# A hybrid attention and mixture-of-experts kernel: Strassen's form for all but three first layers, and three small broadcasts moved from TensorE and VectorE to transfers

## The chip, the cores and the metric

The kernel runs on one core of a Trainium2 chip. The metric is the device time of one execution in microseconds (us), smaller is better; medians of several executions are quoted. A kernel that differs from another by under 2% is classed as "same"; the 95% intervals of the ratios resolve far less than that, so effects of one per cent can still be studied, and this document is about such effects. All executions used here are in the fast state. In the views TensorE is PE (its weight load PEld), VectorE DVE, ScalarE ACT, GpSimd POOL, and SyncE, whose queue issues most transfers, SP. The lines L668 and L669 are those of a helper that records every operation.

## The reference, cut to what matters

The input is 8 maps of 256 channels by 32x32 positions, in f32. Layer 0 is a convolutional attention: queries from every position, keys and values pooled to fewer tokens, 8 heads of 32 channels. Layer 1 is an attention with one head and then 8 experts of three layers, mixed by a gate.

```python
attn = softmax(einsum('bhqd,bhkd->bhqk', q_g, k) * SCALE)      # layer 0
out_att = einsum('bhqk,bhkd->bhqd', attn, v)
...
x = x + _L0_conv_ref(_gn(x), ...)                              # the residual of layer 0
t = _to_tokens(x)
t = t + _L1_attn_ref(_ln_t(t), ...)                            # _ln_t: (v - mean) / sqrt(var + eps), by token
t = t + _L1_ffn_ref(_ln_t(t), ...)
...
h = relu(_bn(einsum('bfd,edh->bfeh', x, W1) + b1, ...))        # experts: first layer
h = relu(_bn(einsum('bfeh,ehk->bfek', h, W2) + b2, ...))       # second
y = einsum('bfeh,ehd->bfed', h, Wo) + bo                       # third
return einsum('bfed,fe->bfd', y, w)                            # w: the gates, softmax over the 8 experts
```

## The kernel before

Layer 0's attention runs in 384 score steps, 12 for each of 32 "units" (8 maps, 2 channel halves, 2 halves of the positions). The work of layer 1 and of the next maps is filling work: TensorE does it in the gaps between score steps. A small model of time inside the program, `Flow`, decides while the program is written in which order every engine gets its instructions. It keeps a clock for each engine, a believed duration for each instruction and a believed landing for each transfer. On the chip each engine then works strictly in that order.

```python
MARGIN = 1.5
NEAR = {"DVE": 1.5, "ACT": 2.0, "POOL": 1.0, "SP": 10.0}
LANDING = 9.5
...
        self.now[engine] = end = start + cost          # in Flow.note, for every instruction
        lag = 0.15
        if "dma" in op:
            lag = 3.0 if engine == "SP" else LANDING    # when a transfer's data are believed there
        for n in {*outs, self.key(out)}:
            self.ready[n] = max(self.ready.get(n, 0.0), end + lag)
...
        if engine == "PE":                              # in Flow.runnable: may a matmul fill this gap?
            until = max(pe, self.free("sc") - 0.5)
            return (... and at + MARGIN <= until and slot <= until)
```

A `yield ve(rec)` in a thread means: go on when `rec` is believed ready for VectorE. The sums of the exponentials and the division by them, in each unit:

```python
            rec = T(work, [P, 512], "rec")              # at the end of sums(n, pairs)
            f.act.activation(rec, total, AF.Copy, accum_out=hi[...])
            return rec

        def normalise(b, c, sl, rec, n):
            att = atts[b, c][:, sl]
            yield ve(rec)
            f.ve.reciprocal(rec, rec)                   # 128 x 512: each of 4 rows stands there 32 times
            f.ve.tensor_tensor(att, att, rec, ALU.mult)
            yield act(rec)
            f.act.activation(rec, rec, AF.Copy, accum_out=lo[...])
```

The reciprocals of the deviations of `_ln_t` (48 broadcasts for the 8 maps), the residual of layer 0, and the gates:

```python
            for g in range(0, tiles, 4):                # in scale_tokens(src, n)
                ...
                f.pool.tensor_tensor(diag, ident[...], r[...], ALU.mult)           # a diagonal for each tile
                yield pe(diag, tag="sm")
                f.pe.matmul(rb[...], lhsT=kit.ones, rhs=diag[...])                 # spreads it over the partitions
                yield ve(rb)
                f.ve.tensor_tensor(d, d, rb[...].to_broadcast([P, 2, m * P]), ALU.mult)
...
                    f.sp.dma_start(xt, x[b, m * P : (m + 1) * P, sl])              # in project(b)
                    ...
                    f.ve.scalar_tensor_tensor(xt, ps, bias[:, m : m + 1], xt, ALU.add, ALU.add)
                    f.sp.dma_start(t1[b][:, m, sl], xt)
...
                for e in range(NE):                     # in gates()
                    f.pe.matmul(ps, lhsT=sel[:, e * P : (e + 1) * P], rhs=gt[:, sl], start=True, stop=True)
                    f.act.activation(gb[:, e, sl], ps, AF.Copy)
```

Of the kernel before, what the change touches and what calls it, by code (L numbers as in the profile page):

```python
# [35 lines left out]
NEAR = {"DVE": 1.5, "ACT": 2.0, "POOL": 1.0, "SP": 10.0}  # L36
BUFS = {"sm": 2, "sx": 1}
PACE2 = 8.0
LANDING = 9.5
# [616 lines left out]
class Flow:  # L656
# [90 lines left out]
    def note(self, engine, op, ins, args, kwargs):  # L747
# [35 lines left out]
        if "dma" in op:  # L783
            lag = 3.0 if engine == "SP" else LANDING
# [95 lines left out]
def attention(tc, kit, f, outer, ended, nb, consts, x, t1, t2, hn, bounds, vecs, q_t, kv_t, proj_t, gqk_t, wqk, wqkv, vecs1, w1_d, w1c, gate_d, wrc, vecs2, bnvec):  # L880
# [6 lines left out]
    with ExitStack() as ctx:  # L887
# [38 lines left out]
        pjw = weight(proj_t, "v", 256, l1)  # L926
# [27 lines left out]
        def mix():  # L954
# [66 lines left out]
            bdt = T(l1, [P, 2, P], "diag4")  # L1021
# [40 lines left out]
        def pool(*tiles):  # L1062
            return "POOL", tiles, None

# [49 lines left out]
        first, large, whole, pooled = {}, [], [], []  # L1114

        def first_diagonals():

            middle = T(l1, [P, 2, P], "rec1")
            rest = T(work, [P, 4, 512], "pt", bufs=6).rearrange("p a (b q) -> p (a b) q", q=P)
            first["diag"] = middle, rest  # L1120
            for c in range(2):
                yield act(vec, mid)
                f.act.activation(middle[:, c, :], ident, AF.Copy, scale=mid[:, c * 4 : c * 4 + 1])
                for i, tap in enumerate((0, 1, 2, 3, 5, 6, 7, 8)):
                    yield act(vec)
                    f.act.activation(rest[:, 8 * c + i, :], ident, AF.Copy, scale=dw(c, 0, tap))

        def first_maps(xp):


            for m in (2, 3, 0, 1):
                c = m % 2
                if m == 2:
                    p, acc = pmap, T(work, [P, NK], "acc", bufs=3)
                elif m == 3:
                    p = T(work, [P, 4, 512], "pt", bufs=6).rearrange("p j q -> p (j q)")
                    acc = T(work, [P, NK], "acc", bufs=3)
                else:
                    both = T(work, [P, 4, 512], "pt", bufs=6).rearrange("p j q -> p (j q)")
                    p = both  # L1140
                    acc = T(work, [P, 4, 512], "pt", bufs=6).rearrange("p j q -> p (j q)")
                for t in (p, acc):
                    if t is not pmap:
                        f.split(t, 512, HW)
                first[m] = p, acc
            for s0, w in KEY_SLICES:
                if s0 >= HW:
                    yield until(lambda: pooled)
                for m in (2, 3, 0, 1):
                    c = m % 2  # L1150
                    p, acc = first[m]
                    src = source(xp, s0, w)
                    yield pe(src, tag="sm")
                    ps = small()
                    for k in range(2):
                        f.pe.matmul(
                            ps[:, :w],
                            lhsT=kvw[:, k, m * P : (m + 1) * P],
                            rhs=src[:, k, :],
                            start=k == 0,  # L1160
                            stop=k == 1,
                        )
                    f.act.activation(p[:, s0 : s0 + w], ps[:, :w], AF.Copy)
                    for s, n in enumerate(SIDES):
                        a, z = max(OFFS[s], s0), min(OFFS[s] + n * n, s0 + w)
                        if a < z and (m >= 2 or s):
                            f.act.activation(
                                acc[:, a:z],
                                ps[:, a - s0 : z - s0],
                                AF.Identity,  # L1170
                                bias=db(c, s),
                                scale=mid[:, c * 4 + s : c * 4 + s + 1],
                            )
                if s0 == 512:
                    large.append("maps")
                    f.spawn(first_keys(), 5)
            whole.append("maps")

        def first_keys():
# [3 lines left out]
            for half in range(2):  # L1183
                for m in range(2):
                    p, acc = first[m]
                    pin = p[:, : n * n].rearrange("p (h w) -> p h w", h=n)
                    yield pe(p[:, : n * n], middle, rest, tag="sm")
                    ps = small()
                    pout = ps.rearrange("p (h w) -> p h w", w=n)
                    for i, tap in enumerate((4, 0, 1, 2, 3, 5, 6, 7, 8)):  # L1190
                        dy, dx, y0, y1, x0, x1 = windows(tap, n)
                        y0, y1 = max(y0, 16 * half), min(y1, 16 * half + 16)
                        f.pe.matmul(
                            pout[:, y0 - 16 * half : y1 - 16 * half, x0:x1],
                            lhsT=rest[:, 8 * m + i - 1, :] if i else middle[:, m, :],
                            rhs=pin[:, y0 + dy : y1 + dy, x0 + dx : x1 + dx],
                            start=i == 0,
                            stop=i == 8,
                        )
                    f.act.activation(acc[:, half * 512 : half * 512 + 512], ps, AF.Identity, bias=db(m, 0))  # L1200
                large.append(("keys", half))
# [135 lines left out]
        def prepare(b):  # L1337

            xi = xs.pop(b) if b in xs else load_x(b)
            st = T(work, [P, 2, 2, 6], "st")  # L1340
# [34 lines left out]
            if b == 0:  # L1375
                todo.extend([None] * 4)
                yield from first_maps(xp)
            else:
                yield from maps(xp)

            for c in range(2):
                if b == 0:
                    qs[b, c] = T(work, [P, HW], "q", bufs=2)
                for half in range(2):
                    sl = slice(half * 512, half * 512 + 512)
                    yield pe(xi, tag="sm")
# [9 lines left out]
                    q = T(work, [P, 512], "pool") if b else qs[b, c][:, sl]  # L1396
# [3 lines left out]
            made[0] += 1  # L1400
# [37 lines left out]
        def keys_and_values(b):  # L1438
            yield until(lambda: b == 0 or len(done) >= 4 * b + 2 and turn[0] >= 2 * b - 2)
            vts[b] = {}  # L1440
            if b == 0:
                for g in range(2):
                    yield from value_tokens(b, g)
            else:
                for g in range(3):
                    f.spawn(value_tokens(b, g), 2)
# [3 lines left out]
            for g in range(2 if b == 0 else 3):  # L1450
                yield from key_tokens(b, g)
            if b == 0:
                yield from value_tokens(b, 2)
                yield from key_tokens(b, 2)
# [32 lines left out]
        def sums(n, pairs):  # L1487
# [16 lines left out]
            return rec  # L1504

        def normalise(b, c, sl, rec, n):
            att = atts[b, c][:, sl]
            yield ve(rec)
            f.ve.reciprocal(rec, rec)
            f.ve.tensor_tensor(att, att, rec, ALU.mult)  # L1510
            yield act(rec)
            f.act.activation(rec, rec, AF.Copy, accum_out=lo[:, column[n] : column[n] + 1])

        def project(b):
# [3 lines left out]
            for m in range(2):  # L1518
                for half in range(2):
                    sl = slice(half * 512, half * 512 + 512)  # L1520
                    if b == nb - 1:
                        xt = last[:, m, sl]
                    else:
                        xt = T(work, [P, 512], "xr")
                        f.sp.dma_start(xt, x[b, m * P : (m + 1) * P, sl])
                    yield pe(atts[b, 0], atts[b, 1], tag="sm")
# [5 lines left out]
                    yield ve(ps, xt)  # L1532
                    f.ve.scalar_tensor_tensor(xt, ps, bias[:, m : m + 1], xt, ALU.add, ALU.add)
                    if b < nb - 1:
                        f.sp.dma_start(t1[b][:, m, sl], xt)
# [4 lines left out]
        def scale_tokens(src, n):  # L1540
# [3 lines left out]
            for g in range(0, tiles, 2):  # L1544
                yield pe(src, tag="sm")
                ps = small()
                for u in range(2):
                    for c in range(2):
                        o = u * C + c * P
                        f.pe.transpose(ps[:, o : o + P], src[:, c, (g + u) * P : (g + u + 1) * P], ident)  # L1550
# [5 lines left out]
            for g in range(0, tiles, 4):  # L1556
                m = min(4, tiles - g)
                yield pool(r)
                diag = T(l1, [P, m, P], f"diag{m}")
                f.pool.tensor_tensor(  # L1560
                    diag,
                    ident[:, None, :].to_broadcast([P, m, P]),
                    r[:, g : g + m].unsqueeze(2).to_broadcast([P, m, P]),
                    ALU.mult,
                )
                yield pe(diag, tag="sm")
                rb = small()
                f.pe.matmul(
                    rb[:, : m * P], lhsT=kit.ones, rhs=diag.rearrange("p t q -> p (t q)"), start=True, stop=True
                )  # L1570
                yield ve(rb)
                d = src[:, :, g * P : (g + m) * P]
                f.ve.tensor_tensor(d, d, rb[:, None, : m * P].to_broadcast([P, 2, m * P]), ALU.mult)
# [3 lines left out]
        def layer1():  # L1577

            for b in range(nb):
# [3 lines left out]
                yield from scale_tokens(t, HW)  # L1583
# [47 lines left out]
        def outputs():  # L1631

            for i in range(4 * nb):
# [41 lines left out]
                f.spawn(norm(b, q, res), 5)  # L1675
# [3 lines left out]
        def norm(b, q, o):  # L1679

            yield from scale_tokens(o, C)
# [108 lines left out]
        def unit(b, c, sl, n, pairs):  # L1790
            rec = yield from sums(n, pairs)
            yield from normalise(b, c, sl, rec, n)
# [10 lines left out]
        f.finish(lambda: key_parts[0] > 1)  # L1803
# [661 lines left out]
```

## Time and profile before

| | before |
|---|---|
| median time | 3413.8 us (3412.5 to 3414.2) |
| profiled span | 3418.4 us |
| PE without a matmul in flight | 213.6 us |
| PE busy at half clock | 114.6 us |

The last two rows are worked out from the trace: the first is the span less the merged records of matmuls, the second the part of those records that lies where the granted clock is 0.5. Full-clock work is busy time less half of the second row: 3418.4 - 213.6 - 57.3 = 3147.5 us. Any change of the span is then a change of one of three things: work, idle time, or half of the half-clock time.

The prediction shows the engine shares, the stages and the start of this kernel. Two more views matter later. First, the start and the steady attention once more, cut at score steps, so that the same pieces of work can be compared (columns: stretch, length, then busy time and instructions of PE, weight load, DVE, ACT and POOL, then granted clock, share of the DMA engines, GB/s). Steps are counted from 0: before's step 8 is at 163 us, step 48 at 341, the last at 1977:

```profile
0.00:163.00 163.00, 105.03 (x380) 49.30 (x384) 98.75 (x253) 65.45 (x112) 42.16 (x64) 0.83 0.23 58
341.00:1977.00 1636.00, 1546.15 (x8776) 694.98 (x8768) 1253.12 (x2169) 1026.45 (x1219) 363.05 (x426) 0.98 0.58 130
```

Second, the waits in that steady stretch (the engine and what it was to write, what ended the wait, then us in total, times, the longest):

```profile
PE sc L669 <- ACT pt L669: 66.2, 66, 3.9
...
DVE pt L669 <- DMA pt<-pt: 62.5, 27, 7.7
DVE rec L669 <- ACT rec L669: 51.9, 20, 5.7
...
ACT p L669 <- DVE acc L669: 31.4, 14, 5.3
```

TensorE's own largest wait is for the exponentials ("pt") that empty its score banks. VectorE waits for transfers where it adds pairs of exponentials that accumulating transfers have summed, and another 31 us for the loads of the residual ("xr", not shown). Before the reciprocals it waits 52 us for ScalarE's copy into "rec". ScalarE (ACT) waits 31 us for VectorE's taps ("acc", the multiply-adds of the convolution on the maps) to free a map buffer.

### The profile page before, as it was taken

How to read it: one execution, taken by the hardware profiler on the slowest of the kernel's cores; microseconds unless marked ns; L12 is line 12 of the kernel's file. 1: busy time of each engine (PE TensorE's matmuls, PEld its weight loads, DVE VectorE, ACT ScalarE, POOL GpSimd, SP SyncE). 2: the span in 40 equal slices, each digit the busy share in tenths (PEclk: the TensorE clock that was granted, in tenths of full speed). 3: DMA queues.
4: the chain of work that ended last, by engine and by line, in shares of the span. 5: the costliest groups of instructions: out<-in, count | busy, mean ns of one | idle time of the engine just before them, and what ended most of it. 6: DMA issues, size and time to landing. Idle time of an engine off the chain costs nothing.

```text
span 3418.4 us, 39922 instructions
## 1 busy us (share of the span) xinstructions
PE 3204.7 (94%) x15264; PEld 1781.8 (52%) x15264; DVE 2285.8 (67%) x3914; ACT 1675.6 (49%) x2193; POOL 499.0 (15%) x616
## 2 busy tenths in 40 slices
PE   7588899999999899999999989998999999999998
PEld 3232244444444334434434356646777777777776
DVE  6587798888888878888644543216776666666665
ACT  3466667566676576566664523342223333333332
POOL 3122213122141221321211200004000000000000
PEclk9699999999999999999999999999999999999999
DMA  1257565555555655555665663123440000000000
GB/s 48 63 114 165 135 135 115 125 126 123 138 116 122 161 108 128 127 122 129 148 134 132 141 191 124 56 77 132 140 160 31 19 29 27 19 19 19 19 13 20
DMA packets 105032, 337.47 MB, mean 99 GB/s; under 512 B 12976, under 2 KB 38328, under 8 KB 81600
## 3 DMA queue, kind: packets, MB, share of 16 engines
q0 software_dynamic: 24576, 172.51, 25.8%
q1 hardware_dynamic: 76896, 160.35, 13.6%
q8 instruction: 122, 2.00, 0.2%
q10 hardware_dynamic: 3360, 1.97, 0.2%
q14 instruction: 78, 0.64, 0.1%
HBM read 98.33 MB, written 63.97 MB: 47 GB/s over the span
## 4 chain that ended last, share of the span: by engine, by line
PE 74%; DMA 5%; ACT 4%; DVE 2%; issue 2%; POOL 1%; SPq 0%; ACTq 0%; DVEq 0%; POOLq 0%
PE bank L669 25%; PE sm L669 18%; PE y L669 11%; PE sc L669 8%; PE sx L669 6%; PE pv L669 6%; ACT pt L669 3%; DMA pt<-pt 2%; DMA t<-xr 1%; DMA xr<-in_x_dram 1%; DVE acc L669 0%; DMA hn<-hn 0%; DVE pt L669 0%; DVE rec L669 0%; DVE xr L669 0%
## 5 line engine op out<-in xcount | busy, mean ns | idle before, releaser
L669 ACT ACTIVATE pt<-sc 128x2048 f32<-128x2048 f32 (+1 forms) x384 | 720.7, 1877 | 317.1 <-PE sc L669 244.7
L669 PE MATMUL sc<-q,kn 32*128 32x512 f32 (+1 forms) x3072 | 452.4, 659 | 115.5 <-ACT pt L669 114.0
L669 DVE SCALAR_TENSOR_TENSOR acc<-p,vec,acc 128x225 f32<-128x225 f32 (+7 forms) x928 | 528.5, 576 | 35.7 <-ACT acc L669 11.2
L669 PE MATMUL bank<-h,w2e 128*128 128x512 f32 x1024 | 480.5, 595 | 0.0
L669 ACT ACTIVATE h<-bank,bnvec 128x512 f32<-128x512 f32 x302 | 233.1, 772 | 484.5 <-PE bank L669 464.4
L669 DVE TENSOR_TENSOR pt<-pt,pt 128x1024 f32<-128x1024 f32 x320 | 390.0, 1261 | 84.8 <-DMA pt<-pt 82.6
L669 PE MATMUL pv<-pt,vt 128*32 128x512 f32 (+1 forms) x3072 | 422.6, 623 | 0.0
L669 ACT ACTIVATE h<-c,bnvec 128x512 f32<-128x512 f32 x210 | 159.6, 807 | 318.6 <-DVE c L669 318.6
L669 POOL DMA_DIRECT2D pt<-pt x192 | 169.8, 884 | 923.2 <-ACT pt L669 788.8
L669 DVE TENSOR_TENSOR c<-p1c,bank 128x512 f32<-128x512 f32 x105 | 72.2, 688 | 314.9 <-PE bank L669 314.9
L669 PEld LDWEIGHTS sc<-q,kn 32*128 32x128 f32 (+1 forms) x3072 | 117.8, 181 | 311.5 <-ACT pt L669 209.4
L669 PEld LDWEIGHTS bank<-h,w2e 128*128 128x128 f32 x1024 | 194.8, 191 | 153.0 <-issue 141.4
L669 PEld LDWEIGHTS pv<-pt,vt 128*32 128x32 f32 (+1 forms) x3072 | 61.0, 109 | 306.6 <-issue 291.4
L669 POOL TENSOR_TENSOR rstd<-rstd,mhalf 128x4 f32<-128x4 f32 (+2 forms) x88 | 107.0, 1216 | 733.8 <-DVE rstd L669 593.7
L669 DVE TENSOR_TENSOR h<-h,gates 128x1024 f32<-128x1024 f32 x128 | 156.9, 1226 | 71.3 <-DMA h<-h 64.2
L669 PE MATMUL bank<-hn,w1e 128*128 128x256 f32 (+1 forms) x604 | 192.7, 448 | 10.1 <-DMA hn<-hn 10.1
L669 PE MATMUL y<-t,s3e 128*128 128x256 f32 x768 | 187.1, 380 | 0.0
L669 PE MATMUL sm<-p,v 128*128 128x256 f32 x736 | 173.8, 388 | 6.1 <-DVE xr L669 6.1
L669 ACT ACTIVATE p<-sm 128x512 f32<-128x512 f32 (+1 forms) x154 | 89.9, 584 | 173.7 <-PE sm L669 134.2
L669 PE MATMUL sm<-y,t 128*128 128x256 f32 x712 | 169.4, 385 | 2.1 <-ACT p L669 2.1
L669 PEld LDWEIGHTS bank<-hn,w1e 128*128 128x128 f32 x604 | 114.7, 191 | 99.9 <-issue 92.4
L669 PEld LDWEIGHTS sm<-p,v 128*128 128x128 f32 x736 | 139.3, 193 | 49.7 <-issue 24.4
(294 smaller groups left out, 4624.9 us busy)
## 6 DMA issues: line engine op xcount, KB each, us to landing
pt<-pt POOLq DMA_DIRECT2D x160, 1024.0 KB, 7.3
h<-h SPq DMA_DIRECT2D x80, 512.0 KB, 3.4
xi<-in_x_dram SPq DMA_DIRECT2D x16, 512.0 KB, 5.0
t<-t SPq DMA_DIRECT2D x8, 1024.0 KB, 6.9
res<-t SPq DMA_DIRECT2D x32, 256.0 KB, 4.4
t<-res SPq DMA_DIRECT2D x32, 256.0 KB, 2.6
hn<-res SPq DMA_DIRECT2D x32, 256.0 KB, 3.4
hn<-hn SPq DMA_DIRECT2D x16, 512.0 KB, 5.8
```

Source lines behind the costliest of these rows:

```text
L669: ins = fn(*args, **kwargs)
```

## The change

The intent is to take work off TensorE and VectorE. (1) First layers of the experts in Strassen's form (7 products of half size in place of 8) from the fourth on. (2) The gates are spread over the partitions by transfers from DRAM. (3) So are the reciprocals of the deviations. (4) The reciprocals of the attention's sums are taken on 16 columns, where each sum stands once, and spread by a chain of transfers. (5) The residual of layer 0 is added by an accumulating transfer. (6) The start is reordered: keys before values, the score loop after one key group. (7) `Flow` believes another landing. The core of the diff:

```diff
-NEAR = {"DVE": 1.5, "ACT": 2.0, "POOL": 1.0, "SP": 10.0}
+NEAR = {"DVE": 1.5, "ACT": 2.0, "POOL": 1.0, "SP": 1.0}
-LANDING = 9.5
...
-            lag = 3.0 if engine == "SP" else LANDING
+            size = ...                                     # KB
+            lag = 2.0 + 0.0045 * size if engine == "SP" else 1.5 + 0.0078 * size
...
             f.act.activation(rec, total, AF.Copy, accum_out=hi[:, column[n] : column[n] + 1])
-            return rec
+            few = T(work, [P, 16], "few")
+            yield sp(rec)
+            f.sp.dma_start(few, rec[::DH, :].rearrange("j (i k) -> j i k", k=16))
+            return rec, few
...
-            yield ve(rec)
-            f.ve.reciprocal(rec, rec)
+            yield ve(few)
+            f.ve.reciprocal(few, few)
+            yield sp(few)
+            f.sp.dma_start(rows[n].rearrange("j (i k) -> (j i) k", k=16), few)
+            yield sp(rows[n])
+            for j in range(4):
+                f.sp.dma_start(rec[DH * j : DH * j + DH, :], rows[n][j : j + 1, :].to_broadcast([DH, 512]))
+            yield act(few)
+            f.act.activation(few, few, AF.Copy, accum_out=lo[:, column[n] : column[n] + 1])
+            yield ve(rec)
             f.ve.tensor_tensor(att, att, rec, ALU.mult)
-            yield act(rec)
-            f.act.activation(rec, rec, AF.Copy, accum_out=lo[:, column[n] : column[n] + 1])
...
-            for g in range(0, tiles, 4):                   # scale_tokens: the diagonals and their matmuls
-                ...
+            yield sp(r)
+            f.sp.dma_start(row.rearrange("o (p u) -> (o p) u", u=tiles), r)
+            yield sp(row)
+            for o in range(0, n, w):
+                rb = T(l1, [P, w], f"rb{w}")
+                f.sp.dma_start(rb, row[:, o : o + w].to_broadcast([P, w]))
                 yield ve(rb)
...
+                        f.act.activation(xt, ps, AF.Identity, bias=bias[:, m : m + 1])
+                        f.pool.dma_start(out=t1[b][:, m, sl], in_=xt, accum_op=ALU.add)
...
-        f.finish(lambda: key_parts[0] > 1)
+        f.finish(lambda: key_parts[0] > 0)
...
+                if i == 4:
+                    f.finish(lambda: {0, 1}.issubset(whole))   # before score step 4: all of this thread's work
...
-                    f.pe.matmul(ps, lhsT=sel[:, e * P : (e + 1) * P], rhs=gt[:, sl], start=True, stop=True)
-                    f.act.activation(gb[:, e, sl], ps, AF.Copy)
+            f.sp.dma_start(gtd, gt)                        # and 16 broadcasts from it, later
...
+            (first if n1 < 3 else first7)(n1)
```

(Cut: the sums around Strassen's products, moved code, the order of the first maps, argument lists.)

## The prediction

> **What bounds the kernel now.** I read the page's engine shares first, then the busy time by stage, then the groups of instructions by shape, then TensorE's waits, then the timeline of the start. The page's first part:
>
> ```profile
> PE 3204.7 (94%) x15264; PEld 1781.8 (52%) x15264; DVE 2285.8 (67%) x3914; ACT 1675.6 (49%) x2193; POOL 499.0 (15%) x616
> ```
>
> TensorE (PE) is busy for 3205 of 3418 us and the chain that ended last is 74% PE. So every matmul taken away should pay almost in full, and everything else can gain only from the 213 us in which PE is idle. Where these lie is in the stretches I cut by stage (columns: stretch, then PE, weight load, DVE, ACT, POOL busy, clock, DMA share, GB/s): start, early attention, steady attention, the experts' two first layers beside the rest of layer 1, and the experts' steady loop.
>
> ```profile
> 0.00:165.00 165.00, 107.03 (x385) 49.66 (x386) 99.44 (x254) 67.05 (x112) 42.16 (x64) 0.82 0.23 57
> 165.00:500.00 335.00, 286.49 (x1646) 107.61 (x1645) 273.89 (x473) 222.02 (x258) 70.97 (x80) 0.95 0.59 131
> 500.00:2003.00 1503.00, 1432.80 (x8126) 660.95 (x8125) 1133.23 (x1954) 928.95 (x1107) 332.38 (x389) 0.98 0.58 129
> 2003.00:2340.00 337.00, 315.04 (x1031) 187.59 (x1029) 95.33 (x174) 109.73 (x174) 36.51 (x55) 0.97 0.33 118
> 2340.00:3418.00 1078.00, 1063.39 (x4080) 775.97 (x4080) 683.93 (x1062) 347.87 (x542) 16.98 (x29) 0.99 0.14 47
> ```
>
> Subtracting, PE is idle 58, 48.5, 70, 22 and 14.6 us. The start is the worst place for its length, and its clock is 0.82. DVE is at 82% from 165 to 500 us and 75% after, so it is the second bound of the attention. In the start's timeline PE has nothing to do until the first keys are in token order:
>
> ```profile
> 75.96 0.66 PE L669 MATMUL sm<-con,pt 128*128 128x128 f32 x4 [1.25 <-ACT vt L669]
> 89.15 1.95 PE L669 MATMUL sx<-con,kt 128*128 128x128 f32 x4 [12.54 <-ACT kt L669]
> 99.73 2.80 PE L669 MATMUL sm<-con,kt 128*128 128x128 f32 x8 [6.38 <-ACT kt L669]
> 102.46 2.09 PE L669 MATMUL sc<-q,kn 32*128 32x512 f32 x8
> 130.28 2.09 PE L669 MATMUL sc<-q,kn 32*128 32x512 f32 x8 [7.14 <-ACT pt L669]
> 145.80 2.09 PE L669 MATMUL sc<-q,kn 32*128 32x512 f32 x8 [6.43 <-ACT pt L669]
> ```
>
> The first scores start at 102 us, and then they stall for 6 to 7 us at a time. The code says why: the start holds all six "pt" buffers (one of diagonals, one for a value map, four for the two key maps and their sums), and the scores' exponentials need the same six.
>
> **What the skill says.** (1) The Trainium skill, "TensorE: Matmul & The Clock Gate", section "What's actually happening": after about 3.4 us of idleness TensorE's clock falls to half. The trace agrees: after the 12.54 us gap the clock reads 0.50 and the same eight score matmuls take 2.09 us, against 1.14 us in warm stretches. (2) "VectorE: DVE Perf Modes", section "First, the fixed hardware budget": a reciprocal is an iterative divide with a repeat count of 8. The trace agrees in direction: 3352 ns for 512 columns against 714 ns for a multiply of that size. (3) "DMA: Bandwidth & Descriptors", section "Anatomy of one DMA": about 2.0 us plus bytes over 436 GB/s. Here 256 KB land in 2.4 to 3.4 us, which agrees; the accumulating 1 MB transfers take 7.3 us against 4.4 by that fit, so for them I take the trace. (4) "SBUF — State Buffer", section "SBUF: two separate sides": GpSimd and a two-input VectorE operation exclude each other. The trace agrees: the 128x128 sums on POOL take 0.45 us alone and up to 1.46 us beside a DVE multiply.
>
> **The change, part by part.**
>
> Matmuls that go. The groups that matter (a matmul in f32 leaves two records):
>
> ```profile
> L669 PE MATMUL bank<-hn,w1e 128*128 128x512 f32 x184 | 84.9, 605 | 10.1 <-DMA hn<-hn 10.1
> L669 PE MATMUL sm<-gt,sel 8*128 8x512 f32 x32 | 15.8, 613 | 0.0
> L669 PE MATMUL sm<-diag,con 128*128 128x256 f32 x48 | 15.4, 403 | 0.0
> L669 PE MATMUL sm<-diag,con 128*128 128x512 f32 x20 | 10.7, 618 | 0.0
> ```
>
> (a) Strassen: 184 records of 512 columns are 23 plain first layers of 4 matmuls each; one takes 3.44 us by the spacing of its records, and a Strassen one, 7 matmuls of 256 columns, 14 records of 0.215 us = 3.01 us. Three stay plain, so 20 x 0.43 = 8.6 us go. The loop's 105 others are Strassen's already. Its price is five DVE sums and one ACT copy for each (about 3.1 us of DVE): 62 us of DVE in a stage where DVE is busy 95 of 337 us. I take it as hidden. (b) Gates: 16 selection matmuls of 0.955 us (a pair every 1.91 us) = 15.3 us, and 16 ACT copies of 0.6 us. In their place come one store and 16 broadcasts of 256 KB. (c) Deviations: 16 broadcasts of 512 columns at 0.86 us and 32 of 256 at 0.43 us (with the sx rows of the same group) = 13.8 + 13.8 = 27.5 us of PE, and the 45 us of POOL that made the diagonals. In place, a small store and a broadcast, about 2.5 us each, with other work beside. PE sum: 8.6 + 15.3 + 27.5 = **51.4 us**, all on the engine that sets the end.
>
> Reciprocals. 32 of 3352 ns (107 us of DVE) become 32 on 16 columns; I estimate 0.2 us each from the 0.17 us of other small DVE operations here. The chain grows by three transfers of about 2.5 us less 3.2 us, some +4 to +5 us for each unit of 12 score steps; a unit takes about 55 us, and the result is wanted only by the end of the next one, so I expect nothing of it on the path. Of the layer-0 residual, 28 DVE additions of 0.75 us become ACT copies of about 0.69 and accumulating transfers. DVE loses about 120 us of attention work, some 7% of the stage. PE's 12.3 us of waits for "xr" (load, add, store, through one buffer) should mostly go, as the load is no longer in that loop.
>
> The start. Keys now come before values, the queries sooner, the loop starts after one key group, and the start's maps leave four of the six pt buffers free. My walk: normalised input at 15 us, 21 us of queries and maps at 1.72 us each, the first key half 15 us of PE, then 12 us of token work, so keys near 64 us; values' taps on DVE from 35 to about 62 us, tokens near 73. Scores start near 70 instead of 102 us, and the eighth step near 105 instead of 150. This does not gain the whole 35 to 45 us, since filling work moves too: of 58 us idle I expect 32 to stay, **26 us**, and **7 us** of slow clock (40 us were worked at about 0.67 from 80 to 160 us).
>
> Early attention, bound by DVE's backlog: 48.5 us idle to 35, **13 us**. Steady attention: 70 to 62, **8 us**. The seam at 2003: a new round of filling work stands before the first expert matmul, which waited 10.1 us for its input, and 7.6 us were lost before the first third layer; 22 to 14, **8 us**. Against these **6 us** for small new waits: the 16 broadcasts are 4 MB ahead of the fetches at the seam, and the last unit's longer chain. Sum: 51.4 + 26 + 7 + 13 + 8 + 8 - 6 = 107, so 3413 - 107 = **3306 us**.
>
> **The rivals.** (A) Only the removed matmuls pay: the waits I hope to shorten reappear elsewhere, since DVE's taps still set when batch 1 has its keys. For it: DVE above 80% early; the pace of the filling work decides PE's gaps. Then 3413 - 51 = 3362 us, within 2%. (B) The synchronous queue becomes the wait: it is one in-order queue and gets about 290 more small transfers, each waiting for a producer; one late producer delays loads behind it. For it: its waits are already hundreds of us. Against: those are mostly waits with nothing due. If each of 32 units cost PE 2 us, 64 us come back: 3370 us. (C) DVE relief is worth more than I say: if early attention is truly DVE's, another 30 us go, 3275 us. (D) Strassen's four banks at once stall the second layer behind slow DVE sums: 20 x 2 us = 40 us, 3345 us. DVE's 28% in that stage speaks against it.
>
> **Range and chances.** A alone or B in part make the high end, 3350; C makes the low end, 3268. The 2% line is 3345 us, which needs 68 us; the matmuls give 51 nearly surely, and the start need add only 17. I give 0.84 to faster by over 2%, 0.14 to within 2%, and 0.02 to slower.
>
> **What would show it.** PE busy near 3145 us (the matmuls and the clock); no records of sel or diag matmuls; 24 records of 512-column first layers; DVE reciprocals of 512 columns gone; first scores before 80 us, and the clock before 165 us above 0.9; the first attention stage's PE idle time near 32 us; the seam near 14. Wrong would be: first scores still after 95 us, PE waits behind few, rows or rb transfers, SP waits of 10 us ahead of loads that are due, or PE idle above 170 us in all.

## The result, and the profile after

| | before | after |
|---|---|---|
| median time | 3413.8 us | 3444.3 us (3438.8 to 3447.9) |
| profiled span | 3418.4 | 3440.4 |
| PE without a matmul in flight | 213.6 | 254.9 |
| PE busy at half clock | 114.6 | 166.6 |
| full-clock work of PE | 3147.5 | 3102.2 |

The ratio is 1.0089, with a 95% interval of 1.0071 to 1.0106. (Here and below a ratio is the mean time of one kernel's fast runs over that of the other's of the same rounds, so it is not quite the ratio of the medians quoted.) The class is "same", but the kernel is 0.9% slower, where I had predicted 3.1% faster.

The accounting says at once where the gain went. Work fell by 45.3 us, as intended. Idle time rose by 41.3 us, and half of the added half-clock time is another 26.0 us: -45.3 + 41.3 + 26.0 = +22.0 us, which is the difference of the profiled spans. (The medians differ by 30.5 us: before's profiled execution, at 3420.2 us, was 6 us slower than its median.) The page's engine line shows the same less sharply, since a slower clock inflates busy time:

```profile
PE 3185.5 (93%) x15256; PEld 1798.4 (52%) x15256; DVE 2197.1 (64%) x3972; ACT 1673.2 (49%) x2225; POOL 474.0 (14%) x596
```

By stage, cut at the same score steps (step 8 at 164, step 48 at 343, last at 2042, first third layer at 2359 us), columns as before:

```profile
0.00:164.00 164.00, 119.08 (x440) 62.46 (x440) 101.42 (x269) 67.45 (x117) 45.05 (x66) 0.87 0.28 76
164.00:343.00 179.00, 140.83 (x828) 45.57 (x824) 124.97 (x229) 114.64 (x127) 24.55 (x30) 0.93 0.63 139
343.00:2042.00 1699.00, 1575.06 (x8840) 714.62 (x8836) 1148.20 (x2169) 1039.12 (x1262) 366.96 (x429) 0.97 0.62 132
2042.00:2359.00 317.00, 285.94 (x1074) 197.06 (x1066) 138.06 (x242) 106.81 (x182) 37.45 (x73) 0.95 0.43 141
```

| stage | idle before | idle after | half clock before | half clock after |
|---|---|---|---|---|
| to step 8 | 58.0 | 44.9 | 30.5 | 29.2 |
| to step 48 | 28.9 | 38.2 | 12.0 | 21.2 |
| to the last step | 89.8 | 123.9 | 59.2 | 92.1 |
| to the third layers | 19.7 | 31.1 | 6.6 | 19.0 |
| the rest | 17.2 | 16.8 | 6.2 | 5.1 |

The steady attention is the place: it takes 63 us longer, its VectorE is 105 us less busy, and TensorE has 34 us more idle time in it. The waits of that stretch, the same view as before:

```profile
PE sc L668 <- ACT pt L668: 94.3, 68, 5.7
DVE few L668 <- DMA few<-rec: 89.7, 20, 9.9
DVE res L668 <- DMA rb<-dev: 87.6, 21, 9.1
DVE pt L668 <- DMA pt<-pt: 85.8, 35, 10.8
...
ACT p L668 <- DVE acc L668: 70.5, 21, 5.5
...
ACT few L668 <- DMA row<-few: 34.1, 11, 10.4
...
DVE t L668 <- DMA rb<-in: 24.6, 9, 4.8
```

Four rows are new. In three of them VectorE stands before the data of the new transfers: 89.7 + 87.6 + 24.6 = 202 us in this stretch, where 52 us for "rec" and 31 us for "xr" have gone. In the fourth ScalarE's accumulation over "few" stands 34 us before the transfer that reads the same buffer. What the smaller reciprocals saved is 32 x (3.35 - 0.25) = 99 us, 0.25 us being their median now. ScalarE's wait for VectorE's taps went from 31 to 70 us, and TensorE's wait for the exponentials from 66 to 94 us. VectorE's own timeline shows how such a wait looks (start, duration, the instruction; in brackets the idle time before it and what ended it):

```profile
544.90 0.25 DVE L668 RECIPROCAL few<-few 128x16 f32<-128x16 f32 x1 [6.89 <-DMA few<-rec]
...
555.44 0.69 DVE L668 TENSOR_TENSOR res<-res,rb 128x512 f32<-128x512 f32 x1 [5.66 <-DMA rb<-dev]
```

A reciprocal of 0.25 us cost VectorE 7.14 us. Its transfer had been issued at 532.2 us, 1.2 us after the residual's new copy of 1 MB on the same queue, and landed 12.8 us after its issue, the longest of all. The Trainium skill, "TensorE: Matmul & The Clock Gate", its table of specifications, says that the queues of ScalarE and VectorE are strictly first in, first out; these rows agree, as nothing that stood behind the 0.25 us went ahead of it.

How long the hops take, as each transfer of such a chain is called here (KB, median us from issue to landing):

```profile
rec<-row SPq DMA_DIRECT2D x128, 64.0 KB, 4.6
...
rb<-in SPq DMA_DIRECT2D x16, 256.0 KB, 4.8
rb<-dev SPq DMA_DIRECT2D x32, 128.0 KB, 4.3
...
row<-few SPq DMA_DIRECT2D x32, 8.0 KB, 1.4
dev<-rstd SPq DMA_DIRECT2D x32, 1.0 KB, 4.5
```

`Flow` believes 2.0 us plus 0.0045 us per KB, so 2.0 to 3.2 us for these. The medians rest on few landings, as not every one can be matched with its issue: 20 of 128, 4 of 16, 6 of 32, 7 of 32 and 2 of 32. The run e1 below has more: 3.2 us for dev<-rstd (25 of 32) and 4.4 for rb<-dev (27 of 32). For the first hop (few<-rec) no landing is listed, but VectorE's waits show it: the 23 reciprocals that waited for it started 1.9 to 12.8 us after its issue, with a median of 4.4. So most hops take 1.5 to 2.2 times what the program believes, and VectorE's instruction is put in its order too early.

A median hides that these hops differ by what is in flight. Of the 23 (those that were waited for, so rather the late ones), 8 had no transfer of 512 KB or more issued in the 6 us before them and took 1.9 us (median), as the program believes; the 15 others took 5.0. That the bulk transfers delay them is not tested by a run. In e10 below it is 2.0 us (6 hops) against 4.1 (13). And of the 103 us that VectorE waited for "few" over the whole run, 29 passed before the transfer was even issued, 26 of them before ScalarE's copy had ended.

The start came earlier and gained nothing. PE's timeline there:

```profile
79.84 1.91 PE L668 MATMUL sc<-q,kn 32*128 32x512 f32 x8 [0.25 <-ACT kn L668]
...
104.06 1.97 PE L668 MATMUL sm<-con,acc 128*128 128x128 f32 x8 [6.11 <-DVE p L668]
...
114.04 0.66 PE L668 MATMUL sx<-con,rec 128*128 128x128 f32 x2 [8.02 <-DVE rec L668]
...
141.48 3.65 PE L668 MATMUL sx<-res,p 128*128 128x256 f32 x8 [4.75 <-DMA res<-in_w_dram]
...
145.06 1.14 PE L668 MATMUL sc<-q,kn 32*128 32x512 f32 x8
```

The first scores start at 79.8 us, where before has 102.5. But from about 96 to 141 us PE works on key groups and on the preparation of layer 1's weights (the matmul with "res" from the weights' DRAM) with 5 to 8 us of waiting at a time, and step 4 stands behind that. Its exponential starts at 146.3 us (before: 128.4), that of step 7 at 157.4 (148.0), that of step 8 at 164.2 (162.7), that of step 48 at 343.3 (340.5).

At the seam to the experts the first expert matmul still waits as long as before (10.1 us), now for its weights:

```profile
2095.16 6.45 PE L668 MATMUL bank<-hn,w1e 128*128 128x512 f32 x8 [9.75 <-DMA w1e<-w1c]
...
2359.03 2.07 PE L668 MATMUL y<-h,wo 128*128 128x256 f32 x4 [8.22 <-DVE h L668]
```

### The profile page after: what moved, and what is told of

It reads as the page before. It is cut to its first block, busy times and chain, and to the rows that moved or that the text cites. A ratio compares the mean times of both kernels' runs of the same rounds, so it can differ in the third digit from the quotient of the medians.

```text
span 3440.4 us, 40576 instructions
## 1 busy us (share of the span) xinstructions
PE 3185.5 (93%) x15256; PEld 1798.4 (52%) x15256; DVE 2197.1 (64%) x3972; ACT 1673.2 (49%) x2225; POOL 474.0 (14%) x596
## 4 chain that ended last, share of the span: by engine, by line
PE 45%; DMA 3%; DVE 1%; ACT 1%; issue 0%; SPq 0%; POOL 0%; DVEq 0%; ACTq 0%
PE bank L668 23%; PE y L668 11%; PE sm L668 5%; PE sx L668 2%; PE sc L668 2%; PE pv L668 2%; ACT pt L668 1%; DMA dev<-rstd 1%; DMA rb<-dev 0%; DMA hn<-hn 0%; DMA feat<-hn 0%; DMA rb<-in 0%; DMA gates<-gtd 0%; DVE pt L668 0%; DMA few<-rec 0%
## 5 line engine op out<-in xcount | busy, mean ns | idle before, releaser
L668 DVE SCALAR_TENSOR_TENSOR acc<-p,vec,acc 128x225 f32<-128x225 f32 (+7 forms) x928 | 517.2, 564 | 31.9 <-ACT acc L668 6.8
L668 DVE TENSOR_TENSOR pt<-pt,pt 128x1024 f32<-128x1024 f32 x320 | 380.3, 1233 | 125.7 <-DMA pt<-pt 116.7
L668 PE MATMUL pv<-pt,vt 128*32 128x512 f32 (+1 forms) x3072 | 430.8, 634 | 4.6 <-ACT att L668 4.5
L668 ACT ACTIVATE h<-bank,bnvec 128x512 f32<-128x512 f32 x262 | 201.4, 770 | 393.1 <-PE bank L668 366.6
L668 ACT ACTIVATE h<-c,bnvec 128x512 f32<-128x512 f32 x250 | 190.1, 808 | 396.8 <-DVE c L668 396.8
L668 DVE TENSOR_TENSOR c<-p1c,bank 128x512 f32<-128x512 f32 x125 | 85.9, 687 | 356.4 <-PE bank L668 356.4
L668 PE MATMUL bank<-t,s1e 128*128 128x256 f32 x750 | 182.3, 379 | 0.0
L668 PEld LDWEIGHTS sm<-p,v 128*128 128x128 f32 x736 | 140.8, 195 | 44.3 <-issue 24.8
L668 PEld LDWEIGHTS sm<-y,t 128*128 128x128 f32 x720 | 132.0, 190 | 53.4 <-issue 32.1
```

The lines of the kernel that those rows point to most:

```text
L668: ins = fn(*args, **kwargs)
```

## The experiments

My theory after this reading: the removed matmuls paid, and the two chains of transfers that VectorE waits for (reciprocals and deviations) ate it, in part because `Flow` believes them twice as fast as they are. Rivals: the transfers' traffic as such; the longer way from the sums to the result; the accumulating residual; the reordered start; and mere luck of the order, since any edit makes `Flow` deal out all later instructions anew. Every kernel below gave correct results. "After" and "before" are the two kernels of this study.

**1. Undo one, the other, or both.** `e1_recip_back` is after with before's reciprocals, `e2_dev_back` after with before's deviations, `e3_both_back` both. The edits put before's code back into after:

```diff
 # e1: in sums and normalise
+            yield ve(rec)
+            f.ve.reciprocal(rec, rec)      # 128 x 512 in place, no few, no rows
             f.ve.tensor_tensor(att, att, rec, ALU.mult)
 # e2: in scale_tokens
+                f.pool.tensor_tensor(diag, ...)
+                f.pe.matmul(rb[:, : m * P], lhsT=kit.ones, rhs=diag..., start=True, stop=True)
 # e3: both
```

> The changed kernel with the layer-0 reciprocals back in place (32 of 3.35 us on VectorE, no few and row transfers); everything else stays. Theory 1 (the new transfers are waited for by VectorE and ScalarE in strict order, 103 us before few and 45 us before the accumulation on few, and that delays the taps and the exponentials): the 107 us of busy return but 148 us of waits go, so the time falls by 5 to 25 us from 3444, to about 3430. Theory 2 (the accumulating residual transfers hold POOL's queue, 166 us of waits for xr): no change, 3440 to 3450. Theory 3 (VectorE is the bound of the attention and the reciprocals' relief was worth having): slower, about 3465.

> The changed kernel with the deviations back on TensorE (diagonals on POOL, ones matmuls, 27.5 us of TensorE), reciprocals still spread. Theory 1: VectorE's waits for rb (107 for the residual's, 27 for the attention input) go and 15 to 45 us come back from them, against 27.5 us of matmuls: 3425 to 3455, about level. Theory 2: TensorE's 27.5 us return in full, about 3470. Theory 3: about 3470 too.

> Both undone: what stays is the new start, the residual by accumulating transfers, the gates by transfers and Strassen from the beginning. Theory 1: all of the new in-order waits go; the attention returns to the pace of the kernel before and the experts keep their gain of some 24 us and a better seam, so 3385 to 3410. Theory 2: the attention stays slow and TensorE's 27.5 us return, 3460 to 3475.

Measured: e1 3403.9 us, ratio to before 0.9972 (0.9961 to 0.9983); e2 3454.9, 1.0121 (1.0104 to 1.0137); **e3 3360.6, 0.9839 (0.9823 to 0.9855)**. e3 beats both kernels. Against after it is 84 us faster; undoing one alone gives -40 and +11 us, so the effects do not add up. e1 and e3 are faster than any theory said; e2 came as theory 1 had it. The steady stretch of e3, and its waits:

```profile
329.00:1966.00 1637.00, 1563.05 (x8902) 713.78 (x8898) 1249.03 (x2174) 1053.00 (x1263) 398.20 (x467) 0.99 0.60 128
```

```profile
DVE pt L668 <- DMA pt<-pt: 111.2, 49, 8.5
...
PE sc L668 <- ACT pt L668: 64.6, 68, 3.0
...
ACT p L668 <- DVE acc L668: 30.8, 12, 4.0
```

VectorE is 101 us busier than in after, over 62 us less of time, and that is the better state: ACT's wait for the taps and PE's for the exponentials are back at before's 31 and 65 us. In e3 idle time is 185.4 us and half-clock time 96.5, in all 28 us and 18 us below before, with 22.0 us less work: 28.2 + 9.0 + 22.0 = 59 us, the difference of its span of 3359.1 us from before's. The price of putting the deviations back is PE work: 3125.5 us in e3 against 3102.4 in e1, 23 us.

**2. A later believed landing for all transfers of the synchronous queue.** `e4_lag`:

```diff
-            lag = 2.0 + 0.0045 * size if engine == "SP" else ...
+            lag = 6.0 + 0.0045 * size if engine == "SP" else ...
```

> The changed kernel with one number of the program's own schedule raised: it believes that a transfer of the synchronous queue lands 6.0 us plus size after issue instead of 2.0, so the instruction that waits for one is placed later in its engine's order; not a single operation or transfer is changed. Theory 1: VectorE's waits for few and rb fall from 237 us to under 80, and the time falls by 15 to 40 us, to about 3415. Theory 2: no change beyond 8 us. If the waits fall and the time does not, theory 1 is wrong about what the waits cost.

Measured: 3484.7 us, 1.0202 (1.0185 to 1.0219): slower (against the line of 2% "unclear"), and the expectation missed. VectorE's wait for "few" over the whole run fell from 103 to 78 us and those for "rb" (107 and 27 us in after) were gone from the list. So the waits fell as expected and the time rose by 40 us, which by the expectation's own words speaks against the theory. But the edit also moved all ordinary loads: the queries' load, which nothing waited for, now held PE for 23 us, and VectorE's wait for the pairs' sums rose from 117 to 204 us. It changed too much to judge the hops by, so I replaced it by the next.

**3. A later believed landing for the hops alone, and three other parts.** `e10_lag_hops` is after with 2.3 us more for the transfers that involve few, the rows, dev, in and sum, so about the medians that the trace shows. `e11_experts_only` is before's attention with after's experts. `e7_project_back` is e3 with before's residual. `e8_unused` is e3 with all the same small transfers (order and sizes kept), the broadcasts going to DRAM that nobody reads; only the synchronous queue waits for them.

```diff
 # e10
+            if any(self.key(a).startswith(h) for a in (out, *srcs) for h in ("few", "row_", "sum_", "dev_", "in_")) ...:
+                lag += 2.3
 # e7
-                        f.pool.dma_start(out=t1[b][:, m, sl], in_=xt, accum_op=ALU.add)
+                    f.ve.scalar_tensor_tensor(xt, ps, bias[:, m : m + 1], xt, ALU.add, ALU.add)
+                        f.sp.dma_start(t1[b][:, m, sl], xt)
 # e8: unused few/rows/rec and row/rb transfers beside before's code
+            f.spawn(unused(n, rec), 0)
+            f.spawn(unused_row(r, n, tiles, row), 0)
```

> The kernel with both parts undone (3361 us) plus the same small transfers in the same numbers and order of dependence, from a constant and from the deviations, spread into scratch memory that no engine reads; only the synchronous queue waits for them. Theory 1 (what costs is that compute engines wait for the results in their order): unchanged, 3355 to 3372. Rival (the synchronous queue is held, or the transfers crowd others): most of the 84 us return, 3400 to 3445.

> The changed kernel, with the landing time that its schedule believes in raised by 2.3 us for the new small transfers alone (few, row, dev, in and their broadcasts), to the 4.5 us that the trace shows; loads are left as they are, unlike in the run that raised all. If misplaced consumers are the cause: VectorE's waits for few and rb drop below 120 us (from 237) and the time falls to 3400 to 3425. If the length of the chain of transfers is the cause: no gain, 3435 to 3470.

> The kernel before with the changed experts alone (Strassen from the beginning, gates by transfers), the attention as before: 23.9 us of matmuls go and the seam may lose up to 7 us more: 3380 to 3392. If the 16 broadcasts of gates stand in the way of the first third layers, 3395 to 3405.

> Both parts undone (3361 us) and the residual too: load, VectorE addition and store, as before, instead of ScalarE copy and accumulating transfer. If the accumulating form pays (VectorE's 21 us, and TensorE's waits for xr): 3370 to 3385. If it costs by holding POOL's queue (166 us of waits for xr): 3335 to 3355.

Measured: e8 3385.6 us, 0.9921 (0.9904 to 0.9937); e10 3404.7, 0.9976 (0.9964 to 0.9989); e11 3387.5, 0.9925 (0.9908 to 0.9941); e7 3372.3, 0.9878 (0.9859 to 0.9898). e11 is 26 us faster than before and has 24.8 us less PE work; the prediction's matmul terms for these two parts were 8.6 + 15.3 = 23.9 us. Its attention keeps before's pace (the last score step is 6 us earlier), so most of the gain lies behind it, where these parts are. e8 lies between the ranges of its two expectations. e10 is 40 us faster than after with nothing changed but beliefs, so the landing belief alone is worth that in this order. Its waits:

```profile
DVE pt L668 <- DMA pt<-pt: 154.1, 63, 7.6
...
PE sc L668 <- ACT pt L668: 101.8, 86, 5.0
...
DVE few L668 <- DMA few<-rec: 44.3, 17, 5.3
...
ACT p L668 <- DVE acc L668: 29.6, 12, 4.5
```

VectorE's wait for "few" halves and those for "rb" fall out of the list, while its wait for the pairs' sums rises from 86 to 154 us; ACT's wait for the taps is back at 30 us. But PE's wait for exponentials does not fall (94 to 102 us). What e10 gained over after is half-clock time (166.6 to 120.0 us, worth 23 us) and 12 us of idle time. So later consumers bring back ACT's wait for the taps, but the link "taps late, so exponentials late" does not carry on to PE's wait in this order.

**4. The belief for each chain alone, and three details.** `e13_recip_lag` is e2 (reciprocals spread) with the hops' later landing, `e14_dev_lag` is e1 (deviations spread) with it. `e15_lag_copy` is e10 with ACT's accumulation over "few" writing another tile, so that it does not hold up the buffer. `e12_no_drain` is e3 without the forced finish before score step 4.

```diff
 # e15
-            f.act.activation(few, few, AF.Copy, accum_out=lo[...])
+            f.act.activation(T(work, [P, 16], "fewc"), few, AF.Copy, accum_out=lo[...])
 # e12
-                if i == 4:
-                    f.finish(lambda: {0, 1}.issubset(whole))
```

> Both parts undone (3361 us), and the forced finish of the keys' taps before the fifth score step taken out. The changed kernel's first scores came 23 us sooner than before (83 against 106 us) but its fifth step 18 us later, as the weights' preparation was pulled into that place. If the forced finish caused that: step 4 comes before 120 us and 5 to 20 us are gained, 3341 to 3356. If the keys' third group sets it anyway at step 8: step 8 stays near 160 us and the time is level, 3356 to 3366.

> Deviations back on TensorE, reciprocals spread, with the landings of the small transfers believed at the measured 4.5 us. It was 3455 without that belief and is 3361 with the reciprocals in place. If misplaced consumers are most of the reciprocals' cost, 3375 to 3400; if the spread of reciprocals costs by its own chain, 3420 to 3455.

> Reciprocals back in place, deviations spread, with the corrected belief. It was 3404 without it and is 3361 with the deviations on TensorE, which does 23 us more work there. Misplaced consumers alone: 3340 to 3365, as TensorE has less to do. If the transfers' presence and chain cost more than the matmuls saved: 3370 to 3400.

> The run with corrected belief (3405 us), with ScalarE's accumulation on few written to another tile, so that it need not wait for the row transfer that reads few (26 us of ScalarE's waits left there). If these waits hold the exponentials: 3385 to 3398. If they fall where ScalarE has slack: 3400 to 3410.

Measured: e12 3363.1 us, 0.9853 (0.9837 to 0.9870); e13 3406.8, 0.9980 (0.9973 to 0.9988); e14 3368.9, 0.9873 (0.9857 to 0.9890); e15 3405.8, 0.9978 (0.9969 to 0.9987). e15 equals e10: that detail is nothing. With the later belief the deviations cost about nothing (e14 is 8 us behind e3) and the reciprocals still cost 46 us (e13 against e3). Both fell between the two ranges of their expectations. e12 shows how the start gives its gain back:

```profile
97.48 1.14 PE L668 MATMUL sc<-q,kn 32*128 32x512 f32 x8 [0.25 <-ACT kn L668]
...
158.74 2.17 PE L668 MATMUL sc<-q,kn 32*128 32x512 f32 x8
```

Without the forced finish step 4's scores come at 97.5 us (in e3 at 141.4) and step 7's at 117.0 (152.9), but those of step 8 only at 158.7, as late as with it (158.8), and the total is level. Keys of the third group are simply not there earlier.

**5. The longer way, and the traffic, by themselves.** `e16_delay` is e3 in which the multiply by the reciprocals is scheduled 25 us later, without any transfer. `e17_unused_recip` is e8 with the unused transfers of the reciprocals alone.

```diff
 # e16
             f.ve.reciprocal(rec, rec)
+            f.ready[f.key(rec)] += 25.0
+            f.writer[f.key(rec)] = "DMA"
+            yield ve(rec)
             f.ve.tensor_tensor(att, att, rec, ALU.mult)
```

> Both parts undone (3361 us), no transfer added; the schedule alone is told that each unit's reciprocals are ready 25 us later, so that the multiply of the attention's output comes some 25 us later in VectorE's order. If the length of the unit's chain is what the spread reciprocals still cost: 3385 to 3410. If it is nothing that others wait for: 3355 to 3370, and the rest must be the waits and transfers themselves.

> Both parts undone, with the unused transfers of the reciprocals alone (32 few, 32 row and 128 broadcasts of 64 KB), not those of the deviations. With both kinds it was 3386. If the reciprocals' transfers make the 25 us: 3378 to 3388. If the deviations' do: 3358 to 3368.

Measured: e16 3395.3 us, 0.9943 (0.9926 to 0.9960); e17 3393.0, 0.9939 (0.9922 to 0.9955). The time from the copy of a unit's result out of its bank to the multiply (median over 32 units, from the trace) is 18.3 us in before, 13.8 in e3, 27.2 in after, 39.1 in e10 and 37.0 in e16. So e16 has e10's delay without its hops, and is 35 us behind e3; e17 has the traffic without delay or waits of the computing engines and is 32 us behind, beyond both ranges that I expected. Both readings depend on how much an order alone can do, which the last runs measure.

**6. The control for the luck of the order.** `MARGIN`, the slack that a matmul must have to be put into a gap, is changed by 0.1 us either way in e3 and in after. This has no meaning for the theory; it only makes `Flow` deal out another order.

```diff
-MARGIN = 1.5
+MARGIN = 1.4      # e18 (from e3), e20 (from after); 1.6 in e19 and e21
```

> Both parts undone (3361 us), with the slack that the schedule asks of a filling task's inputs at 1.4 us instead of 1.5. If the order's luck is small: 3353 to 3370. If 3361 was a lucky order: 3375 to 3395, and then the 25 us of the unused transfers and the 35 us of the delay mean little.

> As the last, with 1.6 us. Small luck: 3353 to 3370; a lucky 3361: 3375 to 3395.

> The changed kernel (3444 us) with the slack at 1.4 us. If its slowness is its parts' and not its order's luck: 3425 to 3460. If it was unlucky: 3390 to 3420.

> As the last, with 1.6 us: 3425 to 3460 if its parts make it slow, 3390 to 3420 if its order was unlucky.

Measured: e18 3386.7 us, 0.9915 (0.9898 to 0.9931); e19 3360.8, 0.9841 (0.9824 to 0.9857); e20 3428.3, 1.0041 (1.0027 to 1.0055); e21 3456.3, 1.0123 (1.0106 to 1.0140). So three orders each:

| | three orders | mean |
|---|---|---|
| e3, e18, e19: neither spread | 3360.6, 3386.7, 3360.8 | 3369 |
| after, e20, e21: both spread | 3444.3, 3428.3, 3456.3 | 3443 |
| e10, e15: both spread, later belief | 3404.7, 3405.8 | 3405 |

An order alone moves the time by up to 28 us. This is the measure that I had lacked for all single comparisons above:

- Shown: the two spreads together cost 74 us, as the slowest of the first row is 42 us below the fastest of the second. Shown too: after's short belief is about half of it. e10 and e15 lie 23 us below the fastest without the later belief and 18 us above the slowest of the first row. (e15 is nearly e10's program, so this is less than two independent orders.) Two more pairs that differ in the belief alone agree: -48 us from e2 to e13 and -35 from e1 to e14, beside -40 from after to e10.
- That the reciprocals are the dearer chain rests on three pairings that agree: e13 against the first row's mean is +37 us, e10 against e14 +36, after's mean against e1 +39. Each alone would be only a little above what an order can do.
- With the later belief the deviations are level: e14 against the first row's mean is 0, e10 against e13 is -2. Their 23 to 27 us of saved PE work are paid back in waits. With the short belief the pairings disagree: e1, one order, is 35 us above the first row's mean, but after's mean is 12 us below e2.
- Not shown: a cost of the traffic. e8 lies within the first row's range and e17 6 us outside it. Nor is the cost of the longer way by itself shown, as e16 is only 9 us above the slowest of the first row. The residual (e7) and the forced finish (e12) are not resolved, nor is what the start, the residual and the other new beliefs are worth together: e11, one order, has none of them and is 18 us above the first row's mean.

The kernel with the shortest time is e3, and e19 shows that it is not one lucky order; its mean over three orders is still 44 us below before.

## Why the prediction was wrong, step by step

**The removed matmuls (51.4 us): right.** Full-clock work fell by 45.3 us. The experts' part was 24.8 us in e11 for 23.9 predicted; the deviations' 23 to 27 us for 27.5. Strassen's extra VectorE sums did not cost the gain: e11, which has them and before's attention, came 26 us under before. Rival D fell with that.

**The reciprocals ("I expect nothing of it on the path") and the deviations ("with other work beside"): the step that failed.** The argument weighed how late the result may come, by a unit's length, and never who stands waiting while it comes. VectorE stands: its queue is in order, and while the small reciprocal waits for the first hop, nothing behind it runs, no taps for the next maps and no sums. Over the whole run it waited 103 us for "few" (in before 65 us there, for the copy into "rec") and 107 and 27 us for the deviations' rows; for the last hop, before the multiply, only 7 us. The smaller reciprocals freed 99 us, and VectorE was not the bound anyway: it has 383 idle us in before's steady stretch (1636 less 1253). That the two chains cost 74 us is shown by undoing them; that VectorE's waits are the way by which they cost it is argued from the traces, and in part only (see what stays open).

**The hops ("about 2.5 us each"): mis-sized, twice.** Where the traces have landings, the medians are 3.2 to 4.8 us, except for the middle hop of the reciprocals (1.4 us, but 5.2 to 10.0 in 3 of 7). Since the program's own belief (2.0 to 3.2 us) was as short, the error was built into the order of every engine. I had quoted a fit of the same form and checked it on transfers of 256 KB that agreed (2.4 to 3.4 us), though the list of before's transfers also has some of 256 KB at 4.2 to 5.7 us. The fit gives what a hop takes with no bulk transfer just ahead of it (1.9 us for the first hop); of the 23 hops that VectorE waited for, 15 had one. Correcting the belief alone gave back about 38 us (3443 to 3405). The chain from the result's copy to the multiply grew by 8.9 us (18.3 to 27.2), where I said 4 to 5.

**The start and the early attention (26 + 7 + 13 us): nothing came.** The first scores came at 79.8 us, 10 us later than I had walked to and barely inside the "before 80" that I gave as a test. The eighth step (step 7, at 148 in before), predicted near 105, came at 157, because of the change's own forced finish before step 4: without it, in e12, step 7's scores come at 117. That gains nothing in all, as steps 8 to 11 need the third key group, which the walk had left out and which still waits for the pooled maps; e12 shows that it comes at about 159 us whatever stands before it. To step 48 idle time is 83.1 us in after and 86.9 in before, half-clock time 50.4 and 42.5: together no gain.

**The steady attention (70 to 62 us, +8) went the other way.** In the stretch cut by steps idle time rose from 89.8 to 123.9 us. A second loss comes with it, which I had counted at the start alone: gaps of TensorE longer than 3 us in this stretch went from 6 (26 us in all) to 10 (43 us), and half-clock time from 59 to 92 us. In e3 one such gap is left, and 37 us at half clock. Over the whole run the added half-clock time costs 26 us; the saved work (45 us) and the added idle time (41 us) nearly cancel.

**The seam (22 to 14 us, +8) went the other way too**, from 19.7 to 31.1 us: the first expert matmul waits 9.8 us for its weights in place of 10.1 for its input, and the third layers 8.2 us for the product with the gates. I did not test this by a run.

**The rivals.** A (the waits reappear elsewhere) was right in kind, but it left the removed matmuls as a gain, and the added waits ate that too. B came nearest in size ("if each of 32 units cost PE 2 us, 64 us come back"), but by another way, a late producer that delays loads. Among the waits of after's steady stretch none for an ordinary load is new; what waits is VectorE, in order, for what the queue brings. e8's and e17's unused transfers through the same queue, 16 and 24 us above the first row's mean, are not clear of an order's luck, so B's part is not excluded. C (VectorE relief is worth more) did not show: VectorE was relieved by 89 us of busy time and the kernel got slower, though what the relief would be worth without the new waits was not tested. My own sign for "wrong", PE idle above 170 us in all, came true with 255.

What stays open: why PE's wait for exponentials stays near 100 us in e10 when ACT's wait for the taps is gone, and how the remaining 36 us of e10 over the first row divide between the longer way and the remaining waits. Since a first hop takes 2.0 us or 4.1 in e10, by what was issued just before it, no one believed landing fits it; a run with the bulk transfers kept away from the hops, the residual's new 1 MB copies first, would test that and was not made.

## What to carry to other kernels

Before an instruction on an in-order engine is exchanged for a transfer, price the exchange as the engine's wait for the landing, not as the length of the transfer "beside other work", and take the landing from the trace of transfers of that kind, with its spread: for 8 KB here 4.4 us on the median, 1.9 with nothing bulky just ahead and up to 12.8 otherwise. Relief of an engine that has idle time need not show in the time, and a program that schedules by beliefs pays for a wrong belief on all engines (38 us here). And before reading effects of under one per cent in such a program, measure what a meaningless change of the order does (28 us here), with two or three orders of each version.

## What the Trainium skill lacked or had wrong

- "DMA: Bandwidth & Descriptors", "Anatomy of one DMA": its 2.0 us plus bytes over 436 GB/s is fitted to transfers issued from GpSimd, and I used it for the synchronous queue. It has no term for other transfers in flight, and no page gives a figure for a small transfer beside bulky ones. Here the first hop, of 8 KB, took 1.9 us, as by the fit, where no transfer of 512 KB or more was issued in the 6 us before it, and 5.0 us (at most 12.8) where one was. For GpSimd's accumulating transfers of 1 MB the trace has 7.3 to 7.6 us against 4.4.
- "VectorE: DVE Perf Modes", "First, the fixed hardware budget": it gives the reciprocal's repeat count but no time. The runs show 3.35 us for 512 columns and 0.25 us for 16.
- No page has a figure for what a transfer costs the in-order engine that consumes it. Here, in one case, 0.25 us of work took 7.1 us of VectorE.
